# Residual rows laid out in DRAM ahead of time, and second-level reads issued by ScalarE, in a two-layer graph-attention kernel

## The chip, the cores and the metric

The kernel runs on one core of a Trainium2 chip. The metric is the device time of one execution in microseconds. Lower is better.

## What is computed

Two attention layers over a graph of N = 2708 nodes with D = 1024 features, all in fp32. `adj` is a 2708 x 2708 matrix of 0 and 1. The reference, cut to what matters:

```python
def layer0(h, adj, Wf, bf, Wg, bg, W, bW):
    f = h @ Wf + bf
    g = h @ Wg + bg
    e = relu(f @ g.T)
    attention = softmax(where(adj > 0, e, NEG), axis=1)
    return attention @ (h @ W + bW)

def layer1(h, adj, W, a1, a2):
    h = h @ W
    e = leaky_relu(h @ a1 + (h @ a2).T, 0.2)
    attention = softmax(where(adj > 0, e, NEG), axis=1)
    return relu(attention @ h)

x = x + layer0(relu(layernorm(x)), ...)     # the residual of layer 0
x = x + layer1(relu(layernorm(x)), ...)
```

A row of attention sums to 1, so the bias `bW` can be added to the residual: x + bW + attention @ (h @ W). The change is about this residual.

## The kernel before, in words

**Tiles.** The rows are cut into 20 tiles of 128, one more of 128 (`MONO`), and one of 20 rows (`TINY`). The attention rows are handled in five panels, laid along the free dimension, 576, 576, 532, 512 and 512 wide. Each large product is made in the seven-product form of fast matrix multiplication on 2 x 2 blocks, whose products are called M1 to M7; tiles go in ten pairs for that. A tile is not 128 rows in sequence: it is four blocks of 32 rows, 128 rows apart in x (`places`, L98). So a tile's residual rows, in two halves of 512 columns, come by eight loads of 32 x 512 (64 KB each), in `load_rows_of` (L278).

**Order of layer 0.** For each panel: `project_q` makes the left operand of its scores; `scores` (L1345) forms the products of pairs of tiles with it (matmuls at L1378) and adds the mask; then come maximum, exp and sums, in pieces; `aggregate` (L890) multiplies the attention by the node rows (matmuls at L661, smaller ones at L927, L931 and L1067; a scale on GpSimd at L977); `project` (L1199) multiplies by W (matmuls at L1267) and, through `finish0`, adds the residual and stores the tile to `x1_d` in DRAM, where layer 1 reads it. Panels 0, 1 and 2 are projected right behind their aggregate, panel 3 where the next panel's `project_q` would be, panel 4 after the loop. The main loop is at L1671 to L1703.

**Small steps.** What VectorE and the stores have to do beside the products is put into lists, `later` and `lazy`, as steps with a cost. The function `behind` runs as many of them behind each product as a rate allows. A step may have a fetch, which is started some steps ahead. `hooks` hang further steps on a product of the seven.

**Second-level sums.** `put_quarters` (L392) reads two pieces of 256 KB of `hr_d` in each of its 35 steps (70 reads), forms sums on VectorE, and stores them to `hs2_d`; the reads are issued by GpSimd (L403). Fetched data are named `hq`. These steps sit in `lazy`, and run only behind the aggregates of panels 1 to 4 (`spare`), and at the end.

**Queues.** `load` (L139) issues on SyncE, in the order of the program. `store` (L143) issues on GpSimd. Instructions that aren't held in program order are ordered by a scheduler by what they depend on. In the built program the DMAs of SyncE and ScalarE share eight completion semaphores, those of GpSimd have eight of their own, and a DMA waits for the one before it that used its semaphore. Loads of 512 KB go through a pool of twelve `stream` buffers; a pool of 54 `slot` buffers holds attention tiles and small things. In the first scores, hs_d is both written, from `hsT` (GpSimd, L143), and read back as `As` (SyncE, L139), through stream buffers of the same pool.

**The residual, `finish0` (L1594).** For each panel it has three parts. `start` loads the rows of some tiles into `x_res`: eight loads on SyncE for each tile; and then, for each half, one accumulating DMA on GpSimd that adds bW, read with a stride of zero so that all rows get it (L1612; L1607 for TINY). `go` adds the product to it on VectorE and stores the tile to `x1_d`. `join` is for a product that has to be added first.

```python
                load_rows_of(t, xs[t], x)
                for e in range(2):
                    nc.gpsimd.dma_start(xs[t][e], bias_of_W(e * W, P, W), accum_op=OP.add)
```

Of the kernel before, what the change touches and what calls it, by code (L numbers as in the profile page):

```python
# [12 lines left out]
OP = mybir.AluOpType  # L13
# [44 lines left out]
def kernel(  # L58
# [66 lines left out]
    def slot(name, shape=(P, WX), dt=FP):  # L125
        return slots.tile(list(shape), dt, tag="slot", name=name)
# [66 lines left out]

    later, lazy, credit = [], [], [0.0]
    ahead = [5]
    spare, from_slots = [False], [False]

    def put(us, go, fetch=None, takes_psum=False, ready=None, to=later):
        to.append([us, fetch, go, takes_psum, ready])
# [192 lines left out]
    def put_quarters(m, k, to=lazy):  # L392

        two = []

        def fetch():
            if from_slots[0]:
                two.extend(slot(f"hq{h}", (P, 2, WH)) for h in range(2))
            else:
                t = stream("hq", (P, 4, WH))  # L400
                two.extend(t[:, 2 * h:2 * h + 2] for h in range(2))
            for h in range(2):
                nc.gpsimd.dma_start(two[h], hr_d[:, m, h, :, k])  # L403

        def go():
            a11, a12, a21, a22 = (two[h][:, i] for h in range(2) for i in range(2))
            add(a22, a21, a22)
            sub(a21, a11, a21)
            sub(a11, a22, a11)
            sub(a12, a12, a11)  # L410
            for h in range(2):
                store(hs2_d[:, m, 2 * h:2 * h + 2, k], two[h])
            made_quarters[m] = made_quarters.get(m, 0) + 1
        put(1.7, go, fetch, to=to)
# [938 lines left out]
    def scores(p, B):  # L1353

        w = width[p]
        h = w // 2
        lo, hi = slice(0, h), slice(h, w)
        fetch, convert, turn = makers[p]
        rb = slot("rb")
        if p == 0:  # L1360
            spread(rb, columns_of(p, r_[:, first_col[p]:]))
        else:
            row_on_all(rb, r_d[p], p)
        acc = slot("acc")
        S = [None] * NT
        rates = (0.6, 1.0, 0.65, 0.65, 0.65)
        lefts = {}

        def product(q, m, ps, start):
            n, i = P, BY_SCORES.index(m)  # L1370
            if i % 2 == 0:
                t = stream("As", (P, 2, NH, P))
                lefts[q] = t
                k = min(2, 7 - i)
                load(t[:, :k].rearrange("p m c j -> p (m c j)"),
                     hs_d[q][:, i:i + k].rearrange("p m c j -> p (m c j)"))
            for c in range(NH):
                nc.tensor.matmul(ps[:n, :h], lefts[q][:, i % 2, c, :n], B[m][c // 2][:, c % 2, :h],  # L1378
                                 start=(start and c == 0), stop=(c == NH - 1), skip_group_check=True)

        def finish(q, s, k):

            n, mk = once(q, k), mk_sb[p, q]
            nc.vector.scalar_tensor_tensor(s[:, :w], s[:, :w], 0.0, mk[:, k, :w], op0=OP.max, op1=OP.add)
            if q == 0 and k == 0:
                nc.vector.tensor_copy(acc[:, :w], s[:, :w])
            else:
                nc.vector.tensor_tensor(acc[:n, :w], acc[:n, :w], s[:n, :w], OP.max)
            if q in known:
                raise_max(p, q, k, mk[:n, k, :w])  # L1390

        def last(q, sb, Z, m1):

            n = P
            product(q, M4, Z, False)
            add(sb[:n, lo], Z[:n, :h], m1[:n, lo])
            finish(q, sb, 1)
            mk_sb.pop((p, q))
            behind(rate, True)

        nc.hold = ("vector",)
        left_over = None
        for q in range(NQ):
            n = P
            make_until(q + 2)
            rate = 1.3 if NQ - 1 not in made else rates[p]
            if q + 2 <= LEFT:
                fetch(q + 2)
            sa, sb = slot("Sa"), slot("Sb")
            S[pairs[q][0]], S[pairs[q][1]] = sa, sb  # L1410
            X, Y, Z = (bank(f"s{k}") for k in "xyz")
            m1, t = slot("sm1"), slot("st")
            product(q, M1, X, True)
            for s in (lo, hi):
                add(m1[:n, s], X[:n, :h], rb[:n, s])
            if left_over:
                left_over()
            product(q, M6, Z, True)
            add(t[:n, lo], Z[:n, :h], m1[:n, hi])
            behind(rate, True)  # L1420
            product(q, M5, Y, True)
            add(t[:n, hi], Y[:n, :h], m1[:n, hi])
            if q + 1 <= LEFT:
                convert(q + 1)
            behind(rate, True)
            product(q, M2, X, False)
            add(sa[:n, lo], X[:n, :h], rb[:n, lo])
            if q + 1 <= LEFT:
                turn(q + 1, 0)
            behind(rate, True)  # L1430
            product(q, M7, Z, False)
            add(sb[:n, hi], Z[:n, :h], t[:n, hi])
            if q + 1 <= LEFT:
                turn(q + 1, 1)
            behind(rate, True)
            product(q, M3, Y, False)
            add(sa[:n, hi], Y[:n, :h], t[:n, lo])
            finish(q, sa, 0)
            behind(2 * rate, True)
            left_over = lambda q=q, sb=sb, Z=Z, m1=m1: last(q, sb, Z, m1)  # L1440

        sm, st = slot("Sa"), slot("Sb")
        S[MONO], S[TINY] = sm, st
        X, Y, Z = (bank(f"s{k}") for k in "xyz")
        m1, zs = slot("sm1"), slot("sz")
        t = stream("As", (P, 2, NH, P))
        load(t.rearrange("p e c j -> p (e c j)"), hsl_d.rearrange("p e c j -> p (e c j)"))

        def part(ps, e, m, start):
            for c in range(NH):  # L1450
                nc.tensor.matmul(ps[:, :h], t[:, e, c], B[m][c // 2][:, c % 2, :h], start=(start and c == 0),
                                 stop=(c == NH - 1), skip_group_check=True)
        part(X, 0, M1, True)
        add(m1[:, hi], X[:, :h], rb[:, hi])
        left_over()

        for c in range(NH):
            for g, (e, m) in enumerate(((0, M1), (1, M2), (0, M5), (1, M3))):
                nc.tensor.matmul(Z[B32 * g:B32 * (g + 1), :h], tinyT[:, e, c], B[m][c // 2][:, c % 2, :h], start=(c == 0),
                                 stop=(c == NH - 1), skip_group_check=True)  # L1460
        nc.scalar.copy(zs[:, :h], Z[:, :h])
        part(X, 1, M2, False)
        add(sm[:, lo], X[:, :h], rb[:, lo])
        behind(rate, True)
        part(Y, 0, M5, True)
        part(Y, 1, M3, False)
        add(sm[:, hi], Y[:, :h], m1[:, hi])
        finish(LEFT, sm, 0)
        for s, pick in zip((lo, hi), picks):
            V = bank("sv")  # L1470
            nc.tensor.matmul(V[:, :h], pick, zs[:, :h], start=True, stop=True)
            add(st[:, s], V[:, :h], rb[:, s])
        finish(LEFT, st, 1)
        mk_sb.pop((p, LEFT))
        behind(rate, True)
        nc.hold = ()
        return S, acc
# [110 lines left out]
        nc.gpsimd.memset(t, 0.0)  # L1588
        return [t[:, e] for e in range(2)]

    def bias_of_W(o, n, k):
        return bass.AP(tensor=bw.tensor, offset=bw.offset + o, ap=[[0, n], [1, k]])

    def finish0(p):  # L1594
        xs, seen = {}, {}

        def start(ts):
            for t in ts:
                if p == NP - 1:
                    first_mask[t] = load_mask(0, *pair_of[t])  # L1600
                if t == TINY:
                    xs[t] = halves_of_tiny("x_res")
                    for e in range(2):
                        for ps, i in by_quarters(x, places[TINY][0][1], e):
                            load(xs[t][e][ps], i)
                        for g, (ps, _) in enumerate(by_quarters(x, 0, e)):
                            nc.gpsimd.dma_start(xs[t][e][ps], bias_of_W(e * W + g * P, NY, P), accum_op=OP.add)  # L1607
                    continue
                xs[t] = row_halves("x_res", t == MONO)
                load_rows_of(t, xs[t], x)  # L1610
                for e in range(2):
                    nc.gpsimd.dma_start(xs[t][e], bias_of_W(e * W, P, W), accum_op=OP.add)  # L1612

        def go(t, e, c):
            add(xs[t][e], c, xs[t][e])
# [53 lines left out]
    for p in range(NP):  # L1669
# [3 lines left out]
        S = got["S"]  # L1673
        hooks = {M1: lambda p=p: take_max(p), M2: lambda p=p: take_softmax(p)}
        if p == 0:
            hooks[M1] = lambda: (take_max(0), sums_until(3))
            sums_h()
        if p + 1 < NP:
            B = project_q(p + 1, hooks)
# [7 lines left out]
        if p == NP - 2:  # L1687
            then[M2] = lambda: first_masks(NP - 1, 0)
            then[M6] = lambda: first_masks(NP - 1, 1)
            then[M7] = lambda: first_masks(NP - 1, 2)  # L1690
        spare[0], from_slots[0] = p > 0, p == NP - 1
        G[p] = aggregate(0, p, S, got["sm"], then)
        spare[0] = False
        if p == 0:
            flush()
            ahead[0] = 2
# [140 lines left out]
```

## Time and profile before

| | |
|---|---|
| runs | 3099.64, 3091.45, 3090.53 us; median 3091.45 |
| the profiled execution | 3099.78 us; its span 3098.0 us, so 1.8 us lie around the span |
| mean granted TensorE clock | 0.989 |
| TensorE (PE) busy | 3002.8 us, 97% |
| VectorE (DVE), ScalarE (ACT), GpSimd (POOL) busy | 2070.7, 463.2, 506.3 us |
| HBM traffic | read 627.95 MB, written 133.91 MB, 246 GB/s |
| residual rows, layer 0 | 160 loads of 64 KB on SyncE (with TINY's 180 in all), 583.9 to 2087.6 us |
| accumulates of bW | 42 of 256 KB on GpSimd (L1612), 599.0 to 2095.2 us, issue 37.0 us in all |
| hq reads | 70 of 256 KB on GpSimd (L403), issue 50.1 us in all |

How to read the profile's lines. The rows of digits cut the span into 40 slices of 77.5 us; a digit is the busy share of an engine in tenths. The DMA row is the mean busy share of the 16 DMA engines. In a timeline a line has the start, the length, the engine, the source line, the operation, its output and inputs by the program's names, the shapes, and how many such instructions are drawn together; in brackets, how long the engine stood idle before it and for what. SPq is SyncE's DMA queue, as the program issues it. In the table of issues the last number is the median time in us from issue to landing.

### The profile page before, as it was taken

What the parts mean: (1) busy time and instruction counts of PE and PEld (TensorE: products, weight loads), DVE (VectorE), ACT (ScalarE), POOL (GpSimd) and SP (SyncE); (2) the same over time, 40 slices, a digit from 0 to 9 for tenths busy, and PEclk for the clock granted to TensorE, in tenths of its full rate; (3) what the DMA queues carried; (4) which work ended last, traced back from release to release, by engine and by line L of the source; (5) the groups of instructions that cost most, each with busy time, mean ns of one, the idle gap of its engine ahead of it and who ended that gap; (6) DMA issues with size and microseconds to landing.
All of it is one profiled execution on the core that took longest, in us unless ns stands there. A gap on an engine that the chain in (4) does not pass through costs nothing.

```text
span 3098.0 us, 41680 instructions
## 1 busy us (share of the span) xinstructions
PE 3002.8 (97%) x14630; PEld 2298.1 (74%) x14630; DVE 2070.7 (67%) x4615; ACT 463.2 (15%) x817; POOL 506.3 (16%) x786
## 2 busy tenths in 40 slices
PE   8998999899999999999999999997999999999998
PEld 4576777657877588885888886783777969879694
DVE  5767693776651596716975277766968768887853
ACT  3420020010110101101011001301222121212200
POOL 1421101310011110214101001141202010020202
PEclk9999999999999999999999999998999999999999
DMA  6999967998565796758967577789667868888896
GB/s 225 291 257 254 301 247 253 309 274 229 178 238 153 217 260 223 244 158 241 278 199 255 164 217 234 237 266 350 229 216 249 274 202 296 287 269 294 264 297 246
DMA packets 448577, 764.70 MB, mean 247 GB/s; under 512 B 175776, under 2 KB 262592, under 8 KB 448368
## 3 DMA queue, kind: packets, MB, share of 16 engines
q1 hardware_dynamic: 393008, 598.31, 62.0%
q0 software_dynamic: 55360, 163.73, 16.4%
q8 instruction: 116, 1.90, 0.3%
q14 instruction: 93, 0.76, 0.1%
HBM read 627.95 MB, written 133.91 MB: 246 GB/s over the span
## 4 chain that ended last, share of the span: by engine, by line
PE 71%; DVE 11%; DMA 7%; issue 7%; SPq 2%; POOL 1%; ACT 1%; POOLq 0%; DVEq 0%; ACTq 0%
PE sz L1378 6%; PE gx L661 6%; PE gy L661 6%; PE gz L661 5%; PE gz L1067 5%; PE pz L1267 4%; PE sx L1378 4%; PE sy L1378 4%; PE px L1267 4%; PE py L1267 3%; PE gx L1067 3%; PE gy L1067 3%; PE M_ps L574 3%; PE qz L661 2%; PE qx L661 2%
## 5 line engine op out<-in xcount | busy, mean ns | idle before, releaser
L1378 PE MATMUL sz<-B,As 128*128 128x288 f32 (+2 forms) x1200 | 293.5, 394 | 11.8 <-DVE st L45 8.8
L1378 PEld LDWEIGHTS sz<-B,As 128*128 128x128 f32 x1200 | 227.8, 191 | 61.8 <-DVE st L45 12.7
L1378 PE MATMUL sx<-B,As 128*128 128x288 f32 (+2 forms) x800 | 199.6, 392 | 6.4 <-DMA As<-hs_d 4.4
L1378 PE MATMUL sy<-B,As 128*128 128x288 f32 (+2 forms) x800 | 199.3, 392 | 2.3 <-DMA As<-hs_d 2.3
L661 PE MATMUL gz<-Sa,hc 128*128 128x288 f32 (+2 forms) x800 | 189.2, 397 | 6.3 <-DMA hc<-hg_d 6.3
L661 PEld LDWEIGHTS gz<-Sa,hc 128*128 128x128 f32 x800 | 153.8, 193 | 40.1 <-DMA hc<-hg_d 6.8
L1378 PEld LDWEIGHTS sx<-B,As 128*128 128x128 f32 x800 | 151.3, 190 | 40.1 <-DMA As<-hs_d 3.7
L1378 PEld LDWEIGHTS sy<-B,As 128*128 128x128 f32 x800 | 152.0, 190 | 33.4 <-issue 2.7
L1067 PE MATMUL gz<-quarter,hc 128*128 128x128 f32 (+2 forms) x1344 | 168.8, 279 | 3.8 <-DVE gT L45 3.7
L143 POOL DMA_DIRECT2D out_dram<-x_res x180 | 89.0, 501 | 482.1 <-DVE x_res L45 474.7
L1067 PEld LDWEIGHTS gz<-quarter,hc 128*128 128x128 f32 x1344 | 160.6, 191 | 5.1 <-DVE gT L45 4.6
L1267 PE MATMUL px<-w,gT 128*128 128x512 f32 x320 | 143.9, 602 | 7.5 <-DMA w<-in_L_gnn_W_dram 6.0
L1267 PE MATMUL pz<-w,ps 128*128 128x512 f32 x320 | 142.1, 594 | 0.8 <-DVE pt L45 0.8
L1267 PE MATMUL py<-w,ps 128*128 128x512 f32 x320 | 142.0, 593 | 0.0
L143 POOL DMA_DIRECT2D mk_d<-mask x55 | 35.8, 652 | 534.8 <-DVE mask L45 528.1
L1267 PEld LDWEIGHTS px<-w,gT 128*128 128x128 f32 x320 | 60.9, 193 | 80.9 <-issue 74.7
L1267 PEld LDWEIGHTS pz<-w,ps 128*128 128x128 f32 x320 | 60.2, 190 | 77.1 <-issue 70.7
L1267 PEld LDWEIGHTS py<-w,ps 128*128 128x128 f32 x320 | 60.5, 190 | 75.8 <-issue 73.9
L574 PE MATMUL M_ps<-wgT,wfT 128*128 128x512 f32 x256 | 113.5, 600 | 1.6 <-ACT hsT L45 1.6
L661 PE MATMUL gy<-T,hc 128*128 128x288 f32 (+2 forms) x480 | 111.6, 394 | 0.0
L977 POOL TENSOR_TENSOR gT<-gT,rr 128x2304 f32<-128x2304 f32 (+5 forms) x12 | 44.4, 3700 | 382.4 <-DVE rr L45 179.8
L661 PEld LDWEIGHTS gy<-T,hc 128*128 128x128 f32 x480 | 91.2, 190 | 19.5
(377 smaller groups left out, 5803.6 us busy)
## 6 DMA issues: line engine op xcount, KB each, us to landing
hc<-hg_d SPq DMA_DIRECT2D x175, 512.0 KB
As<-hs_d SPq DMA_DIRECT2D x150, 512.0 KB
hc<-hr_d SPq DMA_DIRECT2D x119, 512.0 KB
hc<-hs_d SPq DMA_DIRECT2D x112, 512.0 KB
w<-wt_d SPq DMA_DIRECT2D x96, 512.0 KB
w<-in_L_gnn_W_dram SPq DMA_DIRECT2D x72, 512.0 KB
md<-md_d SPq DMA_DIRECT2D x56, 512.0 KB
adj_i<-in_adj_dram SPq DMA_DIRECT2D x200, 128.0 KB
```

Source lines behind the costliest of these rows:

```text
L143: nc.gpsimd.dma_start(a, b)
L574: nc.tensor.matmul(ps, wfT[a][c // NH][:, c % NH, :], wgT[b][c], start=(c == 0), stop=(c == NC - 1))
L661: nc.tensor.matmul(ps[d], left(m, k, d), right(m, k), start=(start and k == 0), stop=(k == K - 1), skip_group_check=True)
L977: nc.gpsimd.tensor_tensor(of(e, s), of(e, s), by(s, k), OP.mult)
L1067: nc.tensor.matmul(ps[:, d], lhs[:, d * P:(d + 1) * P], inner_right(m, n, k), start=(start and k == 0 and d == 0), stop=(k == NK - 1), ski ...
L1267: nc.tensor.matmul(ps, left[i][m][:, k, :], w_[k], start=(start and k == 0), stop=(k == NH - 1), skip_group_check=True)
L1378: nc.tensor.matmul(ps[:n, :h], lefts[q][:, i % 2, c, :n], B[m][c // 2][:, c % 2, :h], start=(start and c == 0), stop=(c == NH - 1), skip_g ...
```

## The change

Three things are changed.

1. The residual with its bias is laid down in DRAM ahead of time. `copy_residual(p)` copies x in tile order to `x1_d`, one DMA from DRAM to DRAM for a tile (512 KB; its outermost dimension is the four blocks). `bias_residual(p)` adds bW to each of those tiles there, one accumulating DMA of 512 KB each. Both are issued by GpSimd. In the program they stand in the scores of the same panel, at pairs 2 and 6; for panel 0 in hooks of the next `project_q`. They are not held in program order.
2. `finish0.start` loads `x_res` from `x1_d`: two loads of 256 KB on SyncE for a tile, in place of eight of 64 KB and two accumulates into SBUF. `go` stores over the same tile of `x1_d` as before.
3. The reads `hq` of `put_quarters` are issued by ScalarE, in program order, while the aggregate of a panel runs in layer 0: 56 of 70. The last 14 remain on GpSimd.

```diff
-                nc.gpsimd.dma_start(two[h], hr_d[:, m, h, :, k])
+                (tc.keep_in_program_order(nc.scalar.dma_start(two[h], hr_d[:, m, h, :, k])) if reads_by_act[0] else
+                 nc.gpsimd.dma_start(two[h], hr_d[:, m, h, :, k]))
...
+            if p and q in (2, 6):
+                (copy_residual if q == 2 else bias_residual)(p)
...
-    def bias_of_W(o, n, k):
-        return bass.AP(tensor=bw.tensor, offset=bw.offset + o, ap=[[0, n], [1, k]])
+    def tiles_of(p):
+        return list(full(p)) + ([MONO, TINY][p - 1:p] if p in (1, 2) else [])
+
+    def copy_residual(p):
+        for t in tiles_of(p):
+            if t < MONO:
+                r = places[t][0][1]
+                nc.gpsimd.dma_start(x1_d[t].rearrange("(g r) c -> g r c", g=P // B32),
+                                    bass.AP(tensor=x.tensor, offset=x.offset + r * D, ap=[[P * D, P // B32], [D, B32], [1, D]]))
+            else:
+                for ps, r in places[t][:1] if t == TINY else places[t]:
+                    nc.gpsimd.dma_start(x1_d[t][:NY] if t == TINY else x1_d[t][ps],
+                                        x[r:r + ps.stop - ps.start, :])
+
+    def bias_residual(p):
+        for t in tiles_of(p):
+            n = NY if t == TINY else P
+            nc.gpsimd.dma_start(x1_d[t], bass.AP(tensor=bw.tensor, offset=bw.offset, ap=[[0, n], [1, D]]), accum_op=OP.add)
...
-                        for ps, i in by_quarters(x, places[TINY][0][1], e):
+                        for ps, i in by_quarters(x1_d[t], 0, e):
                             load(xs[t][e][ps], i)
-                        for g, (ps, _) in enumerate(by_quarters(x, 0, e)):
-                            nc.gpsimd.dma_start(xs[t][e][ps], bias_of_W(e * W + g * P, NY, P), accum_op=OP.add)
                     continue
                 xs[t] = row_halves("x_res", t == MONO)
-                load_rows_of(t, xs[t], x)
                 for e in range(2):
-                    nc.gpsimd.dma_start(xs[t][e], bias_of_W(e * W, P, W), accum_op=OP.add)
+                    load(xs[t][e], x1_d[t][:, e * W:(e + 1) * W])
...
-            hooks[M1] = lambda: (take_max(0), sums_until(3))
+            hooks[M1] = lambda: (take_max(0), sums_until(3), copy_residual(0))
+            hooks[M5] = lambda: bias_residual(0)
...
-        spare[0], from_slots[0] = p > 0, p == NP - 1
+        spare[0], from_slots[0], reads_by_act[0] = p > 0, p == NP - 1, True
         G[p] = aggregate(0, p, S, got["sm"], then)
-        spare[0] = False
+        spare[0] = reads_by_act[0] = False
```

More of the change, by code (lines that the diff above doesn't have):

```diff
@@ L195 @@
     ahead = [5]
-    spare, from_slots = [False], [False]
+    spare, from_slots, reads_by_act = [False], [False], [False]
     def put(us, go, fetch=None, takes_psum=False, ready=None, to=later):
```

## The prediction

> **What bounds the kernel now.** I read the busy times first, then the slices, then TensorE's own timeline for the few places where it stands still, and there the queue of what it waited for.
>
> ```profile
> PE 3002.8 (97%) x14630; PEld 2298.1 (74%) x14630; DVE 2070.7 (67%) x4615; ACT 463.2 (15%) x817; POOL 506.3 (16%) x786
> PE   8998999899999999999999999997999999999998
> DMA  6999967998565796758967577789667868888896
> ```
>
> TensorE works 3002.8 of 3098.0 us, so all that any edit around it can win is the 95.2 us in which it stands still. The change issues no matmul less. Slice 28 (2091 to 2168 us, where layer 0 ends) is the worst of the PE row; its DMA digit is 8. Slices 2 to 4 (77 to 310 us) show the DMA engines at 9: the first scores are made there. TensorE's timeline at the layer change:
>
> ```profile
> 2088.59 3.60 PE L1267 MATMUL py<-w,ps 128*128 128x512 f32 x8
> 2098.14 6.29 PE L1267 MATMUL px<-w,gT 128*128 128x512 f32 x8 [5.96 <-DMA w<-in_L_gnn_W_dram]
> 2104.27 3.60 PE L1267 MATMUL pz<-w,ps 128*128 128x512 f32 x8
> ```
>
> Eight matmuls of this shape take 3.60 us; those after the wait take 6.29 (the granted clock is 0.91 in the window from 2080 to 2120). So the late W costs 5.96 + 2.69 = 8.7 us. SyncE's timeline says why W was late:
>
> ```profile
> 2067.05 0.34 SPq L139 DMA_DIRECT2D maskl<-mk_d  x1
> 2067.84 5.95 SPq L139 DMA_DIRECT2D x_res<-in_x_dram  x8
> 2074.08 0.34 SPq L139 DMA_DIRECT2D maskl<-mk_d  x1
> 2074.70 5.52 SPq L139 DMA_DIRECT2D x_res<-in_x_dram  x8
> 2080.38 0.34 SPq L139 DMA_DIRECT2D maskl<-mk_d  x1
> 2080.83 7.90 SPq L139 DMA_DIRECT2D x_res<-in_x_dram  x8
> 2088.77 1.82 SPq L139 DMA_DIRECT2D w<-in_L_gnn_W_dram  x2
> ```
>
> Four residual tiles, eight loads of 64 KB each, hold SyncE's queue for some 28 us, and W stands behind them.
>
> **What the Trainium skill says.** DMA: Bandwidth & Descriptors, "Issuing engines are not separate DMA queues": the DMAs of ScalarE, SyncE and GpSimd end on the same 16 engines and interleave; another issuer saves only the time to issue. The trace agrees as far as it goes: GpSimd's stores and SyncE's loads share a stretch that is full (below). Same page, "Why a DMA increments its semaphore by 16 and not by 1": a DMA is spread over the largest count up to 16 that divides the outermost dimension of both sides, so the new copies, outermost 4, would use 4 engines. No row of before shows one. Same page, "SWDGE vs HWDGE vs iDMA": accumulating DMAs are GpSimd's alone; the trace has all of them there, and the new biases must stay there.
>
> **The change part by part.** *Removed at the layer change.* The 32 small loads in front of W become 8 of 256 KB. At some 0.4 us of issue each (maskl above: 0.34), they need about 3 us, not 28, so W of product M2 can go some 20 us earlier and be there when TensorE wants it at 2092. That is −8.7 us. The DVE waits after it (8.3 and 3.9 us near 2150) are another chain and stay. In the panels before, the same thinning frees SyncE (20.9 us at 584 in panel 0), but TensorE is busy throughout there: 0. GpSimd loses 42 bias issues, 37.0 us busy with 51.9 us idle before them; nothing on the path waits for them: 0.
>
> *Moved to ScalarE.* 56 of the 70 reads of second-level sums. ScalarE is 15% busy, and in the built order twelve of a panel's fourteen stand after the last exp (panel 1: 867.78 us) and before the first eviction of M1 (880.68). 12 × 0.4 = 5 us fit into the 12.2 us gap. But SyncE and ScalarE share eight completion semaphores in the build, and each DMA waits for the last user of its own, so one SyncE load of a panel waits for a ScalarE read and may come up to 1 us late: 0 to 1 in each of three panels, and behind the waiting load stands all of SyncE's queue. I take +1. GpSimd loses those issues, which hid behind other waits: 0.
>
> *Added.* 22 copies and 22 biases, half a megabyte each, 11 MB and 11 MB. The x rows must still be read from DRAM afterwards, so the copies are extra traffic; the biases take the place of those into SBUF. All are GpSimd's and have no early consumer, and the built order puts them far ahead of where the text does: two copies at the very start; four biases and one copy directly in front of and between the stores hs_d<-hsT of the first scores; five biases at about 350 us; eight copies and eight biases between 600 and 760 us. After 800 us there are none. So the bill comes in the first 800 us, where DMA is fullest. Price of a bias: the issue table shows both kinds at 256 KB.
>
> ```profile
> hq<-hr_d POOLq DMA_DIRECT2D x70, 256.0 KB, 4.2
> x_res<-in_L_gnn_bW_dram POOLq DMA_DIRECT2D x42, 256.0 KB, 7.5
> ```
>
> An accumulate lands in 7.5 us, a plain read of the same size in 4.2, so I count its bytes 1.8 times. For the place I take the windows of 40 us (start, end, length, busy time of five engines with their counts, clock, DMA share, GB/s) and the waits of TensorE in them:
>
> ```profile
> 200.00:240.00 40.00, 40.00 (x187) 31.86 (x186) 32.50 (x74) 9.65 (x18) 9.02 (x17) 1.00 0.91 246
> 240.00:280.00 40.00, 32.53 (x142) 24.79 (x141) 30.53 (x71) 5.80 (x11) 7.58 (x14) 0.96 1.02 282
> 320.00:360.00 40.00, 40.00 (x167) 31.34 (x165) 25.52 (x53) 0.00 (x0) 1.62 (x3) 1.00 0.94 282
> 680.00:720.00 40.00, 36.54 (x149) 27.55 (x148) 33.77 (x72) 0.36 (x1) 5.63 (x9) 1.00 0.96 251
> ```
> ```profile
> 246.00 3.63 PE L1378 MATMUL sz<-B,As 128*128 128x288 f32 x8 [2.38 <-DMA As<-hs_d]
> 253.94 2.21 PE L1378 MATMUL sx<-B,As 128*128 128x288 f32 x8 [2.13 <-DMA As<-hs_d]
> 278.58 2.18 PE L1378 MATMUL sy<-B,As 128*128 128x288 f32 x8 [2.25 <-DMA As<-hs_d]
> ```
>
> From 240 to 280 DMA is full and TensorE already waits for As. As waits for hs_d<-hsT: the chain of waits has such a store at 225.48 taking 11.39 us and then an As load.
> - *At 205 to 240:* 4 × 0.52 MB × 1.8 + 0.52 MB = 4.3 MB, at 282 GB/s 15.2 us. The window before has 0.09 × 40 = 3.6 us of DMA time free. 15.2 − 3.6 = +11.6. Ends: 0 (the biases trickle through beside the stores) and 15.2.
> - *At the start:* TensorE waits for the first weights until 13.56 us. 1 MB of copies at up to 385 GB/s (the window from 5 to 10 us) is 2.7 us; on 4 engines a copy, two sets, twice that: 0 to 5.5. I take +3.
> - *At 350:* five biases, 2.6 × 1.8 = 4.7 MB, 16.7 us, less 2.4 free. But TensorE doesn't wait there, and SyncE fetches ahead in 12 buffers of 512 KB, each of them some 6 us of matmuls: 0 to 14, I take +2.
> - *At 680 to 760:* 16 pieces, 4.2 + 7.5 = 11.7 MB, 41 us of DMA time at 282 GB/s; at shares 0.96, 0.87 and 0.81 the 120 us to 800 have 14 us free. Most is covered by the same buffers: 0 to 20, I take +4.
>
> The rest of the copies lie among 400 to 600 us in panel 0's aggregate, DMA digits 5 to 8: 0, and at most 3 if that cover is gone.
>
> **Sum.** −8.7 + 1 + 11.6 + 3 + 2 + 4 = +12.9 us. The profiled execution took 3099.78 us, of which 3098.0 is the span and 1.8 lies around it; it lies 8.3 us above the median of the runs, 3091.45. 3099.78 + 12.9 = 3112.7, less 8.3: 3104.4.
>
> **Rivals.**
> - *A, the copies and biases are hidden, only the layer change counts.* For it: TensorE is busy 40 of 40 us at 320 to 360 with DMA at 0.94, so a high share alone does not stop it. Against it: the waits for As at 246 to 279. Costs of 0 to 2: −8.7 to −6.7, and up to −12 if waits for residual bias on DVE (2.5 us in all) go too: 3079 to 3085, say 3081.
> - *B, costs and gain cancel.* The burst trickles: at 205 to 240 half its price, 6, at the other places 1 to 3 in all: about 3091.
> - *C, slower, my forecast:* GpSimd's hoisted accumulates in front of hs_d<-hsT delay the stores, so the buffers that SyncE wants for As come free late and TensorE waits longer at 240 to 290. It decides once all added waits together pass 18.0 us (8.7 for the gain, 9.3 for 0.3%); As alone is to give 11.6 of them. With every upper end, 15.2 + 5.5 + 14 + 20 + 3 + 3 − 8.7, +52: not likely together; two of them high gives some +32, 3123.
> - *D, W is late all the same,* since it now waits for a completion semaphore that a ScalarE read holds, behind GpSimd's stores. Then −8.7 is missing: 3113. Against it: in the built order M2's W waits only for earlier loads and for TensorE's products before it.
>
> **Numbers.** A 0.20, B 0.27, C 0.45 with its own range 3100 to 3123, D 0.08. 0.3% (9.3 us) is about what a measurement of this kernel can tell from no change. Faster, below 3082.2: most of A and a little of B, 0.19. Within: the rest of A, B, and the low end of C, 0.31. Slower: 0.50. The range from 3080 to 3123 leaves out A's end and the cases of several upper ends.
>
> **What would show it.** Right: TensorE's wait for W at 2092 gone, with px x8 back near 3.6 us; waits for As at 240 to 300 grown from about 9 us to 20; a store hs_d<-hsT there landing later than the 11.39 us above; the first matmuls at 13.56 a few us later; DMA digits 9 and GB/s up in slices 3 to 10. Wrong: the span shorter by 8 us with the As waits as they were (A); a wait for W still there with x_res no longer ahead of it (D); TensorE idle before hc loads at 870 to 880 by more than 1 us, or ScalarE's m<-gx evictions late, which would make the reads on ScalarE the cause.

## The result and the profile after

The changed kernel takes 3196.56 us (median of 4 runs), the kernel before 3094.51 us (4 runs): 1.0328 times, 95% interval 1.0301 to 1.0354, some 102 us slower. The profiled execution has a span of 3198.7 us. Slower was forecast, but with 3104.4 us and an upper end of 3123: the size is far off.

The page after, busy times and two rows of the slices:

```profile
PE 3022.0 (94%) x14630; PEld 2311.0 (72%) x14630; DVE 2070.9 (65%) x4615; ACT 462.9 (14%) x817; POOL 460.8 (14%) x725
PE   8985979988999999999999999999899999999998
DMA  6887898698948579375793867679686878888796
```

TensorE has the same 14630 instructions and some 19 us more of work, since the granted clock is lower in the long waits (0.55 and 0.65 in the windows below); the rest of the 100.7 us in the span is idle time. Slice 4 of the PE row falls from 8 to 5, slice 6 from 9 to 7. The weak slice at the layer change has gone from 7 (slice 28) to 8 (slice 29; a slice is 80 us long here). The DMA row rises in slices 6 and 7, from 6 7 to 9 8; in slices 2 to 4 it falls from 9 9 9 to 8 8 7.

Since both kernels issue TensorE's instructions in nearly the same order, the lost time can be placed. I counted its instructions in windows of 10 us in both traces, and took the time at which the same count is reached. The difference is the lag of a kernel behind the profiled execution of before (by some 5 us it differs between executions):

| before, us | after | residual part alone | reads alone | copies alone |
|---|---|---|---|---|
| 160 | 5.2 | 3.3 | 0.2 | 4.7 |
| 320 | 49.1 | 51.2 | −1.9 | 37.0 |
| 560 | 65.0 | 66.9 | −4.9 | 38.2 |
| 720 | 88.6 | 86.7 | −4.2 | 51.2 |
| 1200 | 88.9 | 86.1 | −2.1 | 50.1 |
| 1700 | 108.5 | 89.6 | 11.0 | 51.2 |
| 2000 | 108.3 | 89.2 | 11.2 | 50.6 |
| 2200 | 96.7 | 79.3 | 13.5 | 40.9 |
| 3000 | 98.4 | 82.3 | 13.7 | 41.4 |

So the loss is made in three places: the first scores (44 us), the stretch from there to 720 us (40 us), and between 1200 and 1700 us (20 us). The layer change gives back 12. The 44 is a low count. At 190 us the profiled execution of before lost some 7 us in a wait for VectorE that most other kernels don't have, so that at 200 us the kernel after is 2.7 us ahead of it; counted from there, the first scores cost some 52 us.

TensorE's timeline of the kernel after, in the first scores:

```profile
257.70 3.83 PE L1379 MATMUL sx<-B,As 128*128 128x288 f32 x8 [26.70 <-DMA As<-hs_d]
304.29 4.18 PE L1379 MATMUL sz<-B,As 128*128 128x288 f32 x8 [17.92 <-DMA As<-hs_d]
328.43 1.78 PE L1379 MATMUL sy<-B,As 128*128 128x288 f32 x3 [7.43 <-DMA As<-hs_d]
```

These are the waits that took 2 us each before; from 170 to 330 us they add up to 57.4 us, against 9.0. The windows of the first wait, of the work behind it, and of the second wait (columns as in the prediction):

```profile
231.00:257.60 26.60, 0.00 (x1) 0.00 (x0) 5.17 (x11) 1.81 (x3) 3.02 (x6) 0.55 0.94 206
257.60:286.40 28.80, 28.66 (x128) 22.65 (x128) 20.98 (x50) 5.80 (x11) 6.16 (x11) 0.94 0.48 148
286.40:304.20 17.80, 0.00 (x0) 0.00 (x0) 5.48 (x14) 0.00 (x0) 2.18 (x4) 0.65 1.16 229
```

In both waits the DMA engines are busy, 0.94 and 1.16 (the time of a packet is counted where it starts, so a share can pass 1), but they move only 206 and 229 GB/s. Before, with much the same shares, it was 246 GB/s from 200 to 240 us and 282 from 240 to 280. DMA runs dry, at 0.48, only between the waits, while TensorE works. The chain of waits shows how long single transfers took:

```profile
231.67 25.89 DMA As<-hs_d
...
288.15 23.01 DMA adj_i<-in_adj_dram
311.24 17.06 DMA As<-hs_d
```

The load of As that TensorE waits for first was issued at 231.67, so in this wait it is the load's own landing that is late. The stores of hsT are late as well, since GpSimd waits for DMAs of its own to land before it issues them, among them an accumulate:

```profile
239.40 0.54 POOL L143 DMA_DIRECT2D hs_d<-hsT  x1 [3.68 <-DMA x_d<-in_L_gnn_bW_dram]
247.64 1.06 POOL L143 DMA_DIRECT2D hs_d<-hsT  x2 [7.70 <-DMA r_d<-r]
```

From issue to landing such a store takes up to 16.4 us between 215 and 300 us, against 12.5 before.

And at the layer change, SyncE's queue and TensorE:

```profile
2187.16 0.80 SPq L139 DMA_DIRECT2D x_res<-x_d  x2
2188.05 1.07 SPq L139 DMA_DIRECT2D w<-in_L_gnn_W_dram  x2
```
```profile
2197.47 3.60 PE L1268 MATMUL py<-w,ps 128*128 128x512 f32 x8
2200.90 3.60 PE L1268 MATMUL px<-w,gT 128*128 128x512 f32 x8
2204.34 3.60 PE L1268 MATMUL pz<-w,ps 128*128 128x512 f32 x8
```

W is issued 12.9 us before TensorE needs it. There is no wait, and px x8 is at 3.60 again.

### The profile page after: what moved, and what is told of

Its sections match the earlier page's. It is cut to its first block, busy times and chain, and to the rows that moved or that the text cites. A ratio compares the mean times of both kernels' runs of the same rounds, so it can differ in the third digit from the quotient of the medians.

```text
span 3198.7 us, 41275 instructions
## 1 busy us (share of the span) xinstructions
PE 3022.0 (94%) x14630; PEld 2311.0 (72%) x14630; DVE 2070.9 (65%) x4615; ACT 462.9 (14%) x817; POOL 460.8 (14%) x725
## 4 chain that ended last, share of the span: by engine, by line
PE 78%; DVE 10%; DMA 9%; issue 2%; SPq 1%; ACT 1%; POOL 0%; ACTq 0%; DVEq 0%; POOLq 0%
PE gy L662 7%; PE gx L662 6%; PE sz L1379 6%; PE gz L662 6%; PE gz L1068 5%; PE pz L1268 4%; PE sx L1379 4%; PE sy L1379 4%; PE px L1268 4%; PE py L1268 4%; PE gv L662 3%; PE M_ps L575 3%; PE gx L1068 3%; PE gy L1068 3%; PE qx L662 2%; PE qz L662 2%
## 5 line engine op out<-in xcount | busy, mean ns | idle before, releaser
L662 PE MATMUL gx<-Sa,hc 128*128 128x288 f32 (+2 forms) x400 | 98.9, 409 | 10.3 <-DMA hc<-hg_d 10.3
```

Source lines behind the costliest of these rows:

```text
L662: nc.tensor.matmul(ps[d], left(m, k, d), right(m, k), start=(start and k == 0), stop=(k == K - 1), skip_group_check=True)
```

## The experiments

All ratios are to the kernel before on the same chip, with a 95% interval; 0.001 is 3.1 us.

### The parts by themselves

**Residual part only**: the `hq` reads go back to `nc.gpsimd.dma_start(...)`.

> Only the residual part of the change; the second-level reads stay on GpSimd. Theory 1 (the DRAM preparation, issued by GpSimd in the first 800 us, is what costs; the losses that the trace shows at 1300 to 1700 us, some 18 us, are ScalarE's reads): about 3175 to 3185 us, with the wait for W at the layer change gone. Rival (the reads on ScalarE hold up SyncE's queue and are the larger part): below 3130.

Measured: 3189.91 us, 1.0294 (1.0278 to 1.0309). Above the range expected for theory 1, but on its side.

**Reads only**: the kernel before with

```diff
-                nc.gpsimd.dma_start(two[h], hr_d[:, m, h, :, k])
+                (tc.keep_in_program_order(nc.scalar.dma_start(two[h], hr_d[:, m, h, :, k])) if reads_by_act[0] else
+                 nc.gpsimd.dma_start(two[h], hr_d[:, m, h, :, k]))
```

> Only the second-level reads on ScalarE; the residual as before. Theory 1: +10 to +20 us on before, lost in waits for hc in the aggregates of panels 1 to 3; the wait for W at the layer change is still there. Rival: +60 or more. If the prediction's price of the coupling is right, +1 us, within the noise.

Measured: 3115.98 us, 1.0054 (1.0039 to 1.0069), +17 us. It loses them in the aggregates of panels 1 to 3. SyncE's waits, in total (us, times, longest): this line heads the list in this kernel, and the kernel before has none for hq reads:

```profile
SPq L139 <- DMA hq<-hr_d: 159.0, 29, 28.6
```

SyncE's own loads of hc wait until reads that ScalarE issued have landed. ScalarE issues them only behind its last exp. In panel 2, ScalarE, SyncE and TensorE:

```profile
1265.38 0.65 ACT L45 ACTIVATE Sb<-Sb 128x532 f32<-128x532 f32 x1 [0.99 <-DVE Sb L45]
1265.51 9.93 ACTq L45 DMA_DIRECT2D hq<-hr_d  x12
```
```profile
1268.40 26.25 SPq L139 DMA_DIRECT2D hc<-hg_d  x11
```
```profile
1274.92 3.83 PE L662 MATMUL gx<-Sa,hc 128*128 128x266 f32 x16 [1.67 <-DMA hc<-hg_d]
1280.66 3.83 PE L662 MATMUL gx<-Sa,hc 128*128 128x266 f32 x16 [1.92 <-DMA hc<-hg_d]
```

Before, SyncE began this row of hc loads at 1261.56. It is 6.8 us later, and TensorE waits twice. The issue of the twelve reads took ScalarE 9.93 us.

**Copies only**: the accumulates of bW are left out.

```diff
-            nc.gpsimd.dma_start(x1_d[t], bass.AP(tensor=bw.tensor, offset=bw.offset, ap=[[0, n], [1, D]]), accum_op=OP.add)
+            pass
```

> The residual part with the copies, but bW is not added to the residual at all (the accumulates are left out); reads on GpSimd. Theory 1a (the accumulates are the slow part: 13.7 us to landing for 512 KB, and they keep the DMA engines busy): most of the loss goes, about 3100 us or below. Theory 1b (the copies, each on few engines in pieces of 64 KB, are the slow part: 18.9 us to landing at 200 to 330 us): it stays near 3170.

Measured: 3143.41 us, 1.0148 (1.0133 to 1.0163). Neither: the copies carry about half by themselves (+46 us), and the accumulates, added to them, the other 45 (the difference to the residual part). The copies' landing, in the first scores, of this kernel, us min/median/max:

```profile
DMA to landing us min/median/max: 10.2/16.9/23.5
```

**Copies with rows outermost**:

```diff
-                nc.gpsimd.dma_start(x1_d[t].rearrange("(g r) c -> g r c", g=P // B32),
-                                    bass.AP(tensor=x.tensor, offset=x.offset + r * D, ap=[[P * D, P // B32], [D, B32], [1, D]]))
+                nc.gpsimd.dma_start(x1_d[t].rearrange("(g r) c -> r g c", g=P // B32),
+                                    bass.AP(tensor=x.tensor, offset=x.offset + r * D, ap=[[D, B32], [P * D, P // B32], [1, D]]))
```

> The residual part with both, but the copies have their 32 rows as the outermost dimension in place of the 4 blocks, the same bytes in 4 KB pieces; reads on GpSimd. Theory 1b: most of the loss goes, about 3110 us. Theory 1a: within 15 us of the residual part alone.

Measured: 3162.51 us, 1.0204 (1.0187 to 1.0221). This decides nothing on the form: the scheduler gave it another order, with every copy and accumulate ahead of 277 us.

```profile
L1610 POOL DMA_DIRECT2D x_d<-in_L_gnn_bW_dram x22: 795/908/1777, 34.8 to 276.3; - x22
```

Its lag is 19 us at 160, 74 at 240, and no more after that. All the work at the front costs 74 us in its first 240.

### The place, and the form of a copy

**Held in place**: every copy and accumulate wrapped in `tc.keep_in_program_order(...)`, so that they stand where the program has them; reads on GpSimd.

> The residual part alone, reads on GpSimd, but copies and biases are held where the program text puts them (panel 0's behind the exp steps of the next project_q, the others' at pairs 2 and 6 of the panel's own scores). Same transfers, same sizes. Theory 2 (it is the hoisting into the first 330 us and around 400 and 650 us, where DMA is full or where the first scores hang on freshly stored tiles, that costs): most of the 91 us of the residual part goes, about 3100 to 3115 us, no wait for As above some 3 us at 200 to 330. Rival (the extra traffic costs wherever it lies): 3160 us or more.

Measured: 3149.53 us, 1.0161 (1.0144 to 1.0179). The lag at 320 us is 0.0 in place of 51. So the hoisting is 41 us of the 91, but 50 remain: 20 us from 320 to 480, where the copies and accumulates of panel 0 now stand (in the next `project_q` and at the start of panel 0's aggregate), and in the scores of the later panels 9 near 800, 12 up to 1200 and 14 up to 1600; 10 come back at the layer change. Both theories were too simple.

**Held, rows outermost**: the two edits together. Here the places are the same.

> As the held one, with the copies' 32 rows outermost in place of the 4 blocks, so that they come in 4 KB pieces and can be spread over all engines; they stand at the same places here. If a copy on few engines holds up every other transfer that has a share there, this is faster than the held one, by some 5 to 15 us; if only bytes count, the same.

Measured: 3119.55 us, 1.0066 (1.0050 to 1.0081): 29 us less, for the form of 20 copies alone.

**Held, 4 blocks outermost, short pieces**: two copies of 512 columns for a tile.

```diff
+                for e in range(2):
+                    held(nc.gpsimd.dma_start(x1_d[t][:, e * W:(e + 1) * W].rearrange("(g r) c -> g r c", g=P // B32),
+                                             bass.AP(tensor=x.tensor, offset=x.offset + r * D + e * W, ap=[[P * D, P // B32], [D, B32], [1, W]])))
```

> As the held one, with each tile's copy in two halves of 512 columns: the outermost dimension of the source is still the 4 blocks, but the pieces are 2 KB in place of 64 KB. If it is the count of engines that a copy is spread over which costs the 30 us between the two held kernels: near the held one, some 3140 to 3155 us. If it is the long pieces: near the one with rows outermost, 3115 to 3125 us.

Measured: 3136.57 us, 1.0127 (1.0113 to 1.0140). In between: of the 29 us, some 10 go with the long pieces and 19 with the outermost 4. The split is rough, since this kernel also has 40 copies in place of 20, and two of them are in flight together. The Trainium skill (DMA: Bandwidth & Descriptors, "Why a DMA increments its semaphore by 16 and not by 1") says that an outermost 4 means 4 engines; no view here counts engines, but the time agrees with it. The landing of the copies in the three held kernels (4 blocks, 512 KB; rows outermost, 512 KB; 4 blocks in short pieces, 256 KB):

```profile
DMA to landing us min/median/max: 9.2/11.1/12.2
DMA to landing us min/median/max: 5.8/9.0/13.4
DMA to landing us min/median/max: 6.3/9.9/14.1
```

A copy of the 4-block form lands only 2 us later than one with rows outermost, and still 20 of them cost 29 us more. So what it costs is not its own landing; that it holds up the transfers beside it is the likely reading, and no run shows it directly.

### The accumulates

**Held, rows outermost, no bias.**

> The held copies with rows outermost, and no bias: bW is not added to the residual at all. Theory: what is left of the loss there, some 18 us at 800, 1200 and 1600 us, is the accumulates', about 26 against the 8 that the layer change gives, so that this ends at or below before, 3085 to 3100 us. Rival: the copies' bytes cost the same, 3105 us or more.

Measured: 3085.78 us, 0.9969 (0.9960 to 0.9978). The copies are free in this form and place; the accumulates in DRAM are 30 us (1.0066 − 0.9969).

**Accumulates of other rows**, and **bW written, not added**:

```diff
+            held(nc.gpsimd.dma_start(x1_d[t], bass.AP(tensor=x.tensor, offset=x.offset + min(t, 19) * P * D, ap=[[2 * D, n], [1, D]]), accum_op=OP.add))
```
```diff
+            held(nc.gpsimd.dma_start(x1_d[t], bass.AP(tensor=bw.tensor, offset=bw.offset, ap=[[0, n], [1, D]])))
```

> The held kernel with rows outermost, but its 22 accumulates add other rows of x (every second row, all different) in place of bW, so the output is another. If the accumulate itself (reading both operands and writing) is slow: the same as with bW, 3115 to 3125 us, 14 us to landing. If it is that all 128 rows read the one row of bW: near the one without bias, 3085 to 3095 us, landing in 7 us or less.

> The held kernel with rows outermost, but bW is written over the rows and not added (the residual is lost). If reading one row of bW 128 times is what is slow: the same as with the accumulate, 3115 to 3125 us. If it is the accumulate: near the one without bias, 3085 to 3095 us.

Measured: 3117.64 us, 1.0052 (1.0038 to 1.0065), and 3102.32 us, 1.0006 (0.9997 to 1.0014). That all rows read one row of bW makes no difference that these runs can tell. A plain write at these places costs 11 us, adding makes it 26 to 30 (each against the held kernel without bias). In the lag of the held kernel with rows outermost, the accumulates lose 9 us in panel 1, 13 in panel 2, 2 in panel 3 and nothing clear in panels 0 and 4; the DMA shares that stood there before (0.87 and 0.81, then 0.90 and 0.94) don't tell which.

**Copies in DRAM, bias in SBUF** as before, the whole computation:

> All residual rows copied in DRAM, held in place and with rows outermost; bW is added to them in SBUF as the kernel before does; all reads on GpSimd. The computation is whole. If copies of this form are free and the accumulates into SBUF were free before: about as fast as the held one without bias, 3083 to 3090 us, the wait for W gone. Rival (the wait for the SBUF bias takes the place of what was won): the same as before.

Measured: 3098.59 us, 0.9994 (0.9986 to 1.0002), no difference. The rival holds in its number: the lag falls by 7.5 us up to 2100 and rises again by 5.5 up to 2200, where the eight accumulates into SBUF now fall among the loads of W. What TensorE waits for is W; that the accumulates beside it are the reason is likely, since the held kernel without bias keeps its gain of some 10 us there:

```profile
2105.50 1.34 PE L1267 MATMUL py<-w,ps 128*128 128x512 f32 x2 [3.62 <-DMA w<-in_L_gnn_W_dram]
```

### The layer change by itself

**W first**, in the kernel before:

```diff
-        ws = {m: load_W(l, m) for m in order[:2]}
+        ws = {m: load_W(l, m) for m in order[:3 if by_pair and l == 0 else 2]}
```

> The kernel before, with one edit: in panel 4's project of layer 0 the W of the third product (M2) is loaded ahead of the residual rows, not behind them. No DRAM preparation, no reads on ScalarE. If the wait for W at 2092 us is due to the residual loads ahead of it in SyncE's queue alone: 3.5 to 9 us below before, about 3087, with px x8 back at 3.6 us. Rival (something else is late next: the next W, or the residual rows themselves at M2's eviction): the same as before within 3 us.

Measured: 3103.3 us, 1.0007 (1.0000 to 1.0014), no gain. The wait for M2's W is gone, and the next W takes its place:

```profile
2100.68 5.43 PE L1267 MATMUL pz<-w,ps 128*128 128x512 f32 x8 [7.32 <-DMA w<-wt_d]
2109.35 1.10 PE L1267 MATMUL py<-w,ps 128*128 128x512 f32 x2 [3.24 <-DVE ps L45]
```

**Residual rows of panel 4 on GpSimd**, nothing in DRAM:

```diff
-                load_rows_of(t, xs[t], x)
+                if p < NP - 1:
+                    load_rows_of(t, xs[t], x)
+                else:
+                    for e in range(2):
+                        for ps, r in places[t]:
+                            nc.gpsimd.dma_start(xs[t][e][ps], x[r:r + ps.stop - ps.start, e * W:(e + 1) * W])
```

> The kernel before, with one edit: panel 4's residual rows are loaded by GpSimd in the same 64 KB pieces, not by SyncE, so that none stands ahead of any W in SyncE's queue. Nothing is laid down in DRAM. If SyncE's queue is the cause of the wait at 2092 us: 6 to 10 us below before, as with panel 4's rows prepared in DRAM. Rival: GpSimd's 32 issues and eight biases, in order behind the hq reads, bring the residual too late for M2's eviction, and the wait goes over to VectorE: before or up to 10 us above.

Measured: 3107.31 us, 1.0034 (1.0022 to 1.0047). The rival: rows and biases come too late by way of GpSimd, and TensorE waits on VectorE.

```profile
2110.91 2.07 PE L1267 MATMUL py<-w,ps 128*128 128x512 f32 x2 [13.80 <-DVE pt L45]
```

**Only panel 4 prepared in DRAM**, held in place, rows outermost, bias included; panels 0 to 3 as before.

> Only panel 4's four tiles are prepared in DRAM, held in place in panel 4's scores, copies with rows outermost; the other panels' residuals and all reads as before. If the gain at the layer change is real and 4 MB of transfers are free there: 5 to 10 us below before, about 3086. If the copies and biases cost where they lie too: the same as before or up to 10 us above.

Measured: 3091.44 us, 0.9974 (0.9960 to 0.9987), 8 us below before. It computes everything, and it is the only such version here whose interval lies below 1, though it is faster by less than the 0.3% named in the prediction.

### What made the first scores so dear

**Four copies among the stores of hsT**, in two forms. The base is the held kernel with no bias.

```diff
+            if p == 0 and q in (1, 2, 3, 4):
+                copy_residual(1, [full(1)[q - 1]])
```

> The held copies with rows outermost and no bias (bW is not added), but four of the copies, those of panel 1's full tiles, are put into the first scores at pairs 1 to 4, among the stores of hsT, where the changed kernel has its hoisted ones. If a copy spread over all engines costs its bytes: 4 times 0.52 MB at 282 GB/s, at most 8 us above the held one without bias (3086). If any transfer at this place starts the chain of late stores, late As and late TensorE work: 30 us or more above.

> The same, with those four copies alone in the changed kernel's form, the 4 blocks outermost. Theory: here a copy that sits on few engines holds up every store and load that has a share there, so this loses 25 to 45 us against the held one without bias, as the copies did in the kernel with copies only, and most of it at 220 to 330 us. Rival: it loses no more than its twin with rows outermost.

Measured: 3092.36 us, 0.9985 (0.9976 to 0.9994), and 3099.37 us, 1.0011 (1.0004 to 1.0018). Against the base (0.9969) that is +5 us for the place and +8 more for the form: each as expected in sign, but 13 us in all, far from the 41 that the kernel with copies only lost there (its lag goes from −3.8 at 200 to 37.0 at 320 us). My theory falls short. The 8 is no clean figure either: with the first form the scheduler left two small stores r_d<-r in this stretch (at 223.7 and 268.3 us), with the second it moved them to 343 us. Still, the second form brings one wait of the long kind, with no r_d store near:

```profile
272.75 4.12 PE L1378 MATMUL sx<-B,As 128*128 128x288 f32 x8 [15.23 <-DMA As<-hs_d]
```

**The r_d stores.** The new order on GpSimd also moves four small stores, pieces of 4 bytes, in between the hsT stores; in the kernel after they landed 18.4 to 22.5 us after their issue.

```diff
+            if p == 0 and q == 1:
+                for s_ in (1, 2):
+                    columns_to_row(r_d[s_], s_, r_[:, first_col[s_]:])
```

> The kernel before, with no copy and no accumulate in DRAM; the four small stores r_d<-r of panels 1 and 2 (pieces of 4 bytes) are moved from their early places to behind the first hsT store of pair 5 in the first scores, where the changed kernel's new order has them. The r_d stores of panels 3 and 4 go behind the first scores. If these moved stores, a side effect of the new order, are what holds up the stores and loads there: 15 to 40 us above before, lost at 220 to 330 us. Rival (they are small and cost nothing; the copies do it): the same as before within 5 us.

> The kernel with four copies of the 4-block form in the first scores (bW not added), with the r_d stores moved in the same way. If the 41 us that the kernel with copies only lost there come from both together: 25 to 40 us above its twin, 3125 to 3140 us. If neither: within 5 us of its twin.

Measured: 3093.2 us, 0.9992 (0.9984 to 1.0001), and 3100.56 us, 1.0016 (1.0008 to 1.0023). In sum the moved stores cost nothing, so by themselves at this place they are not the 41 us. But these edits also took the two r_d stores of panels 3 and 4 out of the stretch (before, at 229.47 and 266.84 us), and the traces show that such a store is not cheap. In the kernel before, one of 2 KB was issued at 117.97 and landed at 129.0 us; the windows in front of it, until it landed, and behind:

```profile
108.00:118.00 10.00, 10.00 (x37) 5.41 (x36) 6.48 (x18) 4.11 (x9) 4.36 (x9) 1.00 0.92 333
118.00:129.00 11.00, 11.00 (x30) 4.97 (x30) 9.79 (x22) 3.21 (x8) 4.51 (x8) 1.00 1.03 143
129.00:139.00 10.00, 10.00 (x35) 5.22 (x34) 7.20 (x18) 5.73 (x11) 3.55 (x7) 1.00 1.03 371
```

While it is under way, the DMA engines are as busy and move less than half. The two kernels with four copies of the 4-block form show the same: from 218 to some 232 us they move 309 GB/s without r_d stores there, and 183 with them. In both cases TensorE worked on without a pause, so nothing was lost at once. The kernel with only the r_d stores moved issues the other two at 601 us. Until they land, with two accumulates under way beside them, the rate is 65 GB/s, and TensorE waits behind that:

```profile
601.00:612.00 11.00, 11.00 (x27) 4.94 (x26) 7.75 (x11) 3.12 (x5) 3.74 (x5) 1.00 0.67 65
618.16 8.80 PE L1267 MATMUL py<-w,ps 128*128 128x512 f32 x16 [4.53 <-DMA w<-wt_d]
```

Its lag rises by 6 us there, after it had fallen by some 5 from 240 to 560. So its sum of nothing may well be a gain in the first scores and a loss here. In the kernel after, the three long waits of the first scores stand right behind r_d stores (issued at 225 to 231, 284.7 and 310.5 us), and directly behind each of these a copy is issued (231.2, 285.5, 311.3). The last kernel has such a pair once, at 222 us; TensorE waits 5.2 us some 15 us later, but this kernel loses no more than its twin, so the pair alone is not enough; no run rebuilt all three with the kernel's other traffic around them. This explanation is left open; the wait of 15.23 us above shows that copies of this form can hold up As without it.

## Why the prediction was wrong

**What bounds it, and the layer change: right.** −8.7 us was forecast; the kernel with panel 4 alone prepared gains 8. The lag of the kernel after falls by 11.6 from 2000 to 2200 us. But "W can go some 20 us earlier" was not the whole reason: with W moved alone the next one was late, and with the bias left at its place the gain was mostly given back. The gain needs both the 32 loads and the eight accumulates out of that stretch.

**ScalarE's reads: the mechanism right, the size wrong.** The prediction named the shared completion semaphores, and took "0 to 1 in each of three panels", +1. It measured +17. The mistake was to price one wait of one load. SyncE waits 29 times for such reads, 159 us in all; the reads start 4 us behind where SyncE had begun its own row, and one or two hc tiles of a panel come late.

**At the start, +3: about right.** The lag at 160 us is 5.2 after, 3.3 with the residual part alone.

**"At 205 to 240", +11.6: the step that failed most.** The place and the victim are right (As behind hs_d<-hsT, the stores held up by accumulates), but the size is 44 to 52. The sum turned bytes into time at 282 GB/s, 1.8 us for a copy, and charged the delay once. In the waits the DMA engines were as busy as before, 0.94 and 1.16, and moved 206 and 229 GB/s; and the wait came three times, 26.7, 17.9 and 7.4 us. The first and longest hangs on a load of As that was already issued at 231.67, and not on a store, so the path of the prediction is only a part of it. Nor are the accumulates, which make up most of the sum, needed for the loss: the kernel with copies only loses 41 us there, with three copies that the sum would price at 1.8 us each. The prediction also quoted the rule on the outermost 4 and used it only for the copies at the start. In the held kernels the form of the copies is 29 us, at other places; in the first scores the one pair of runs gives 8.

**Its signs.** TensorE's wait for W is gone, an hsT store takes longer than 11.39 us (16.4), and the first matmuls start later (18.00 us in place of 13.56), all as forecast. The waits for As were to grow to 20 us and grew to 57. DMA digits were to go up in slices 3 to 10 and did so only at 6 and 7.

**"Most is covered by the same buffers", +2 and +4: wrong.** From 320 to 560 us the lag grows by 16, from there to 720 by 24. Part of the 16 lies where the prediction put 0 for the copies from 400 to 600 us; it read the DMA digits there as 5 to 8, but they are 6, 7 and 9. In the held kernels, too, accumulates in the scores of panels 1 to 3 cost, where DMA shares of 0.81 to 0.94 had looked like cover. A likely reason, not tested by itself, is that twelve buffers don't help when a buffer comes free only with a store or load that is itself late.

**An accumulate as 1.8 times its bytes: somewhat low.** Written plainly it costs 11 us in all, added 26 to 30, so 2.3 to 2.7 times as much.

The residual part, then, in terms that were measured: −10 (held copies, no bias) + 30 (accumulates in DRAM) + 29 (form of the copies) + 41 (hoisting) = 90 us, against 91 measured. These terms are differences along a chain of runs, so their sum comes near 91 by construction, and with another order the terms would differ: with the hoisted copies the accumulates are 45 us, with the held ones 30. The reads add 17 alone, 10 on top of it.

**The rivals.** A and B (costs hidden, or equal to the gain) fall for the kernel as it is; B's kind of balance is what the copies with the bias in SBUF show. D falls, since W is early. C holds in part (stores are held up by accumulates), with its price wrong.

**Open:** what makes up the 41 us of hoisting in detail. It is a net figure: hoisted, the kernel loses some 51 us more up to 320 us and some 10 less afterwards. The kernel with copies only loses 41 us in the first scores, too, but that is another 41; four copies put at the same place cost 13. What stands first among the untested is an r_d store with a copy directly behind it. The changed order moves also hg_d and mk_d stores there, and the landing of adj loads on which SyncE's later loads wait; these weren't moved one by one.

## What to carry to other kernels

A transfer without an early consumer is not free: before adding one, look where the built program puts it, and hold it in place if the scheduler may float it to a stretch that feeds itself through DRAM. Price it by what it delays and not by its bytes, and give its access pattern an outermost dimension that spreads it. When a queue is cleared for one late load, ask at once which load is late next.

## What was not expected of the hardware

A copy from DRAM to DRAM of 512 KB lands in 9.0 us with 32 rows outermost and in 11.1 us with the 4 blocks outermost, yet 20 of the latter cost this kernel 29 us more. While a store of 2 KB in pieces of 4 bytes was under way, for 11 us, the rate of all transfers was 143 GB/s at a DMA share of 1.03, against 333 just before. DMA engines at shares of 0.94 to 1.16 moved 206 and 229 GB/s in the waits above, and 282 at 1.02 in the kernel before. Reading one row of 4 KB for all 128 rows of an accumulate was no slower than reading 128 different rows (1.0066 and 1.0052, intervals overlap).
